# Four-layer graph network: layer 1 prepared in three blocks beside layer 0's output projection, and row norms applied without their scale

## The chip, the core and the metric

The program runs on one core of one Trainium2 chip. A core has five engines that each work through their own instructions in order: PE (TensorE, matrix products and transposes; its weight loads are shown as PEld), DVE (VectorE), ACT (ScalarE), POOL (GpSimd) and SP (SyncE, which here issues DMAs). They wait for each other through semaphores. PE writes to eight PSUM banks; everything else is in SBUF or in the chip's main memory. The metric is the device time of one execution in microseconds (us); lower is better.

## The reference

The input is `x`, 3327 nodes of 128 features, and `adj`, a sparse weighted 3327 x 3327 matrix. Four layers follow each other, each of them as `x = x + layer(relu(layernorm(x)), adj)`; the norm has no weights: `(x - mean) / sqrt(var + 1e-5)`.

- Layer 0: attention with 128 heads of 8 features, with 2 x `adj` added to the scores before the softmax, and an output projection with `Wo`.
- Layer 1 (hyperbolic): `h = exp0(log0(x) @ embed)`, a hyperbolic addition of a bias, `neigh = exp0(adj @ log0(h))`, then the same kind of product with `layer` on `[x, neigh]`. `exp0` and `log0` scale each row by a function of its length (`tanh(n)/n`, `artanh(n)/n`), so every row needs the sums of squares of several vectors.
- Layer 2 (hyperbolic): `adj @ logmap0(...)` on rows made in the same manner from `x @ weight.T` and a bias, with clips to the ball.
- Layer 3: `A_norm @ X @ W_in + A.T_norm @ X @ W_out`, each with the inverse degrees of its direction.

So layers 1 to 3 need four products of `adj` (or its transpose) with a 3327 x 128 matrix.

## The kernel before

**Attention (to about 10281 us).** Scores, exponentials and products for 128 heads; the result goes to main memory as `oT_d`, 9 values per head and node: 8 sums and the softmax's denominator. The change does not touch this part.

**The last part** works on 26 tiles of 128 nodes (`NT = 26`), kept in SBUF as `xs`. Two blocks, `BLOCKS = (range(0, 16), range(16, 26))`, are prepared one after the other.

*Output projection* (lines 1095 to 1115). For each tile, `f_load` brings 9 x 128 x 128 values from `oT_d` (odd tiles on POOL's queue, even ones on SP's) to one of four buffers `f_ot`, which borrow space in `uT` and `w1`. `f_norm` divides by the denominators on DVE (a reciprocal and a product, L1101 and L1102), `f_turn` makes eight transposes on PE (L1108) that ACT copies back (L1109), and `f_mul` makes eight products with `woT` (L1114), whose sum DVE adds to `xs` (L1115). The loop at line 1317 issues the norm two tiles ahead and the turn one tile ahead of the product. `load_nodes` (line 830) loads all of `x` on SP between the first tile loads.

*Chains.* Work beside the main loops is written as generators. `start` puts one in a list, `tick(us)` lets the first of the list issue its next pieces until their stated costs (the numbers that they yield) have used up `us`, and `drain` issues the rest at once. This decides at build time where an instruction stands on each engine; at run time every engine takes its own in that order.

*Preparing a block* (`pre1` for layer 1, `pre2` for layer 2): statistics of each tile on DVE (`layer_norm`, L926 and L927), the inverse deviation `r`, `relu(r x - r mean)` per tile on ACT (L933), squares on ACT and their sums on DVE (`row_squares`, L917 and L919), a chain of some 25 small DVE operations on `[128, tiles]` with a square root and a logarithm on ACT, transposes of the tiles by PE (L941) and copies to `hT` by DVE (L942), products with the layer's weight (`project`, L961), whose result `take_a` copies and squares on ACT, a second chain of some 45 small operations with four functions on ACT, and `spread` (L974 and L912), which makes the tiles `y`. ACT loads a table before a function of another set (L185).

*Aggregation* (`aggregate`, line 1021). For each of 26 strips of 128 rows of `adj` or its transpose, PE multiplies tile `y[t]` with the strip's chunks of 512 columns (L1035), and `tick` follows every chunk. In some aggregations DVE also sums the strip for the degrees (L1039). `feed` loads strips into a pool of six buffers, on SP and POOL in turns. A strip's buffer is free once PE and the degree sum are through with it.

The order is: projection with `pre1` of block 0 beside it and drained after it; aggregation of layer 1 over block 0's columns, with `pre1` of block 1 beside it, drained before strip 16; its second half, with `post1` and `pre2` of block 0 beside it, drained after it; layer 2's first half with `post1` and `pre2` of block 1 beside it, drained before strip 16; and so on to layer 3. The lines that set the start of layer 1 are these:

```python
        if t == first[-1]:
            drain()
            start(pre1(0))
        tick(1.1)
        if t >= NT - 4:
            feed(t - NT + 5)
```

## Time and profile before

| | us |
|---|---|
| median of 3 runs (11112.82 to 11114.44) | 11113.94 |
| the profiled execution | 11115.08 |
| its span | 11113.3 |
| output projection's first transposes of a tile | 10297.90 |
| first aggregation's first product | 10429.53 |
| PE waits before layer 2's first product | 15.30, until 10621.68 |
| PE waits before strip 16 of that aggregation | 14.22, until 10701.16 |

The page gives busy times over the whole span: ACT 10187.7 us (92%), PE 10706.3 (96%), DVE 8565.0 (77%). These are mostly the attention's. For the part that the change touches, stretches of the last 832 us have to be asked for. In a timeline a line has the start, the time that a run of equal instructions took, the engine, the line of the kernel, the operation, what it writes and reads, their number, and in brackets how long the engine was idle before it and who ended that. `SPq` is SP's queue of DMA issues. An `issue` in brackets means that the profile shows no wait that ended there. Starts of following lines tell the cadence, which is shorter than the durations where instructions overlap. A transpose or a product may be recorded in one or two pieces, so counts are twice the number of products for L1114, L961 and L1035.

### The profile page before, as it was taken

The page shows a single profiled execution, that of the slowest core. Times are in us where ns is not written, and L with a number is a line of the kernel's source. Part 1 is how long each engine was busy: PE and PEld are TensorE (multiplying, and loading weights), DVE is VectorE, ACT ScalarE, POOL GpSimd, SP SyncE. Part 2 cuts the span into 40 slices and gives each one's busy share as a digit, 9 for nine tenths or more (in the row PEclk, how much of TensorE's full clock was granted, in tenths as well). Part 3 has the DMA queues.
Part 4 walks back from the last instruction along what each step waited for, and adds up shares of the span by engine and source line. Part 5 has one row for each costly group of instructions (what it writes and reads, how often), then busy time and mean ns, then how long its engine had stood idle before and what let it go on. Part 6 is the DMA issues. An engine that isn't in the chain of part 4 may idle for free. (4 is left out here: it accounts for less than half of the span.)

```text
span 11113.3 us, 205604 instructions
## 1 busy us (share of the span) xinstructions
PE 10706.3 (96%) x72876; PEld 3602.0 (32%) x72876; DVE 8565.0 (77%) x13863; ACT 10187.7 (92%) x13845; POOL 2014.2 (18%) x3149
## 2 busy tenths in 40 slices
PE   4599999999999999999999999999999999999889
PEld 2233333333333333333333333333333333333544
DVE  5588887888878887788887888878887777777655
ACT  3599999999999999999999999999999999999330
POOL 5111111111111111111111111111111111111101
PEclk7799999999999999999999999999999999999899
DMA  8855555555555554555555555565555554443668
GB/s 248 253 95 90 96 96 103 97 96 88 96 110 90 95 96 78 110 96 88 96 88 112 96 96 86 90 119 89 94 88 88 104 85 80 84 84 65 195 234 281
DMA packets 683025, 1243.40 MB, mean 112 GB/s; under 512 B 188050, under 2 KB 543401, under 8 KB 668943
## 3 DMA queue, kind: packets, MB, share of 16 engines
q1 hardware_dynamic: 631724, 1100.76, 51.5%
q0 software_dynamic: 50272, 129.37, 4.1%
q8 instruction: 590, 9.67, 0.4%
q14 instruction: 439, 3.60, 0.2%
HBM read 1082.90 MB, written 146.60 MB: 111 GB/s over the span
## 5 line engine op out<-in xcount | busy, mean ns | idle before, releaser
L659 ACT ACTIVATE e<-S 128x952 f32<-128x952 f32 (+1 forms) x9408 | 8702.4, 1150 | 13.0 <-PE S L647 10.4
L700 PE MATMUL po<-e,VA 128*9 128x476 f32 (+1 forms) x46592 | 5738.4, 564 | 19.8 <-DVE OS L708 2.9
L640 DVE TENSOR_TENSOR S<-a,shb 128x476 f32<-128x476 f32 (+1 forms) x5824 | 4026.9, 691 | 1769.4 <-ACT e L659 1307.6
L647 PE MATMUL S<-QS,KT 64*128 64x476 f32 (+1 forms) x23296 | 4841.3, 447 | 50.5 <-DVE S L640 24.3
L647 PEld LDWEIGHTS S<-QS,KT 64*128 64x128 f32 x23296 | 2410.1, 183 | 5143.4 <-ACT e L659 1473.3
L662 ACT ACTIVATE e<-S 128x476 f32<-128x476 f32 (+1 forms) x3808 | 2363.0, 760 | 3.8 <-PE S L647 3.5
L682 DVE SCALAR_TENSOR_TENSOR e<-e,h 128x476 f32<-128x476 f32 (+1 forms) x2016 | 1388.3, 689 | 46.2
L712 POOL DMA_DIRECT2D oT_d<-OS x896 | 470.8, 531 | 4788.5 <-DVE OS L708 4742.9
L566 POOL TENSOR_SCALAR QS<-QS 32x476 fp32r<-32x476 f32 (+1 forms) x1344 | 986.6, 734 | 1470.0 <-DMA QS<-qS_d 798.3
L700 PEld LDWEIGHTS po<-e,VA 128*9 128x9 f32 x46592 | 690.8, 88 | 1607.3 <-issue 1514.0
L1035 PE MATMUL pu<-strip,y 128*128 128x512 f32 (+2 forms) x1456 | 600.6, 567 | 44.8 <-issue 29.2
L673 DVE TENSOR_SCALAR h<-S 128x476 f32<-128x476 f32 (+1 forms) x672 | 439.1, 653 | 78.7 <-PE S L647 5.6
L684 DVE SCALAR_TENSOR_TENSOR e<-e,h 128x476 f32<-128x476 f32 (+1 forms) x672 | 442.7, 659 | 0.0
L677 DVE TENSOR_TENSOR h<-h,h 128x476 f32<-128x476 f32 (+1 forms) x672 | 442.5, 658 | 0.0
L682 DVE SCALAR_TENSOR_TENSOR e<-h 128x476 f32<-128x476 f32 (+1 forms) x672 | 438.9, 653 | 0.0
L576 POOL COPY VA<-VR 128x832 f32<-128x832 f32 x224 | 223.6, 998 | 958.2 <-DMA VR<-v_d 644.9
L1035 PEld LDWEIGHTS pu<-strip,y 128*128 128x128 f32 (+1 forms) x1456 | 272.9, 192 | 322.4 <-issue 288.5
L675 DVE TENSOR_SCALAR h<-h 128x476 f32<-128x476 f32 (+1 forms) x672 | 318.7, 474 | 23.2
L679 DVE TENSOR_SCALAR h<-h 128x476 int32<-128x476 f32 (+1 forms) x672 | 279.2, 415 | 23.0
L1039 DVE TENSOR_REDUCE deg<-strip 128x1 f32<-128x1536 f32 (+3 forms) x104 | 192.8, 1881 | 77.7 <-DMA strip<-in_adj_dram 41.0
L987 ACT COPY uT<-pu 128x512 f32<-128x512 f32 (+1 forms) x21 | 11.2, 553 | 244.3 <-PE pu L1035 244.3
L291 DVE STREAM_TRANSPOSE cols<-rows 128x416 f32<-128x416 f32 x208 | 204.3, 987 | 21.2 <-DMA rows<-in_adj_dram 13.6
(240 smaller groups left out, 2050.6 us busy)
## 6 DMA issues: line engine op xcount, KB each, us to landing
KT<-kS_d SPq DMA_DIRECT2D x1792, 208.0 KB
KT<-kS_d SPq DMA_DIRECT2D x1792, 104.0 KB
VR<-v_d SPq DMA_DIRECT2D x224, 416.0 KB
QS<-qS_d SPq DMA_DIRECT2D x3072, 14.9 KB
QS<-qS_d SPq DMA_DIRECT2D x1536, 29.8 KB
adjT<-cols SPq DMA_DIRECT2D x26, 1664.0 KB
a<-adjT SPq DMA_DIRECT2D x156, 238.0 KB
rows<-in_adj_dram SPq DMA_DIRECT2D x309, 104.0 KB
```

The source lines that it names most:

```text
L566: nc.gpsimd.tensor_scalar(QS[b][r0:r0 + 32, j + 1, :w], QS[b][r0:r0 + 32, j, :w].bitcast(F32), -1.0, 0.0, op0=ALU.mult, op1=ALU.add)
L640: touch(u, [r], nc.vector.tensor_tensor(bank(u, r), adj_of[c][2 * q + r][:, :w], shift_of[c][:, :w], op=ALU.subtract))
L647: x = nc.tensor.matmul(bank(u, r), KT[b][64 * r:64 * r + 64, max(0, j - 1), q * P:(q + 1) * P], QS[b][64 * r:64 * r + 64, j, :w], start=Fa ...
L659: touch(u, (0, 1), nc.scalar.activation(e[:, :, :w], S[:, odd:even + 1, :w], AF.Exp, scale=2.0))
L662: touch(u, [r], nc.scalar.activation(e[:, 1 - r, :w], bank(u, r), AF.Exp, scale=2.0))
L673: touch(u, [1], nc.vector.tensor_scalar(f, bank(u, 1), LOG2_E2, EXP_LEAST, op0=ALU.mult, op1=ALU.max))
L677: nc.vector.tensor_tensor(f, f, whole, op=ALU.subtract)
L682: nc.vector.scalar_tensor_tensor(e, f if k == 4 else e, EXP_C[k], f, op0=ALU.add, op1=ALU.mult)
L684: nc.vector.scalar_tensor_tensor(e, e, EXP_C[0], power.bitcast(F32), op0=ALU.add, op1=ALU.mult)
L700: nc.tensor.matmul(po[32 * j:32 * j + H + 1, :w], VA[k % 2][:, 2 * pairs[v][2] + of, j, :], e_of[v, j][:, 1 - of, :w], start=(q == 0 and r ...
L712: nc.gpsimd.dma_start(oT_d[:, d * N + c * CW:d * N + c * CW + w], o[32 * j:32 * j + H + 1, :w])
L1035: nc.tensor.matmul(got[c][:, :k], y[:m, t, :], s[:m, c * 4 * P - c0:c * 4 * P - c0 + k], start=(t == 0), stop=(t == NT - 1))
```

## The change

- The norm of layers 1 and 2 is made by a new function `centred` in place of `layer_norm`, `squared` and `turned`. DVE only subtracts the mean and clips at zero; the scale `r` is left out, and put in later, on small values: sums of squares are multiplied by `r * r`, the projection's dot product and the coefficient of `a` by `r`, and the copies of the other projection (`keep1`) by `r` of their row. Every four tiles it transposes, copies to `hT` on ACT and squares. In `pre2` the additions of `post1` are made inside the same loop, tile by tile.
- `pre1` is run for tiles 0 to 7, 8 to 15 and 16 to 25. The first two are started at the projection's tiles 7 and 15, and the loop's `tick` is 3.5 in place of 1.1.
- The projection has eight tile buffers; four are strips' buffers, borrowed from the pool of six. Tile loads and node loads are issued in another order, and strips are fed from three tiles before the end of the loop instead of four.
- `row_squares` becomes `square_of`: the sum over a group's squares is issued after the next group's square. Its tile has six buffers.

`layer_norm` stays in use for layer 3.

```diff
-    def load_nodes():
-        nc.gpsimd.memset(xs[96:P, NT - 1, :], 0.0)
-        nc.sync.dma_start(xs[:, 0:13, :], node_rows(x, 0, 13))
-        nc.sync.dma_start(xs[:, 13:NT - 1, :], node_rows(x, 13, NT - 1))
-        for p0, p1 in pieces(P - 1):
-            nc.sync.dma_start(xs[p0:p1, NT - 1, :], x[(NT - 1) * P + p0:(NT - 1) * P + p1])
+    def load_nodes(t0, t1):
+        m = min(t1, NT - 1)
+        nc.sync.dma_start(xs[:, t0:m, :], node_rows(x, t0, m))
+        if t1 == NT:
+            nc.gpsimd.memset(xs[96:P, NT - 1, :], 0.0)
+            for p0, p1 in pieces(P - 1):
+                nc.sync.dma_start(xs[p0:p1, NT - 1, :], x[(NT - 1) * P + p0:(NT - 1) * P + p1])
...
-    def row_squares(sm, dst, ts, rows):
-        sq = part.tile([P, 4, P], F32, name="sq")
+    late = deque()
+    def reduce_late(k=0):
+        while len(late) > k:
+            late.popleft()()
+    def square_of(ts, rows, sm, dst):
+        sq = part.tile([P, 4, P], F32, name="sq", bufs=6)
         nc.scalar.activation(sq[:, :len(ts), :], rows, AF.Square)
         t0 = sm.own[0]
-        nc.vector.tensor_reduce(dst[:, ts[0] - t0:ts[-1] + 1 - t0], sq[:, :len(ts), :], axis=AX.X, op=ALU.add)
+        late.append(lambda: nc.vector.tensor_reduce(dst[:, ts[0] - t0:ts[-1] + 1 - t0], sq[:, :len(ts), :],
+                                                    axis=AX.X, op=ALU.add))
+        reduce_late(1)
...
-    def turned(h):
-        def go(ts):
+    def centred(sm, h, add=None):
+        ts = sm.own
+        mv = wts.tile([P, len(ts), 2], F32, name=f"{sm.pre}_mv")
+        sm.hh = sm.new()
+        for four in fours(ts):
+            for t in four:
+                if add:
+                    add(t)
+                st = part.tile([P, 6], F32, name="st", bufs=8)
+                nc.vector.bn_stats(st, xs[:, t, :])
+                nc.vector.bn_aggr(mv[:, t - ts[0], :], st)
+                nc.vector.tensor_scalar(h[:, t, :], xs[:, t, :], mv[:, t - ts[0], 0:1], 0.0, op0=ALU.subtract, op1=ALU.max)
+                yield 1.4 if add else 0.7
             ps = next_bank()
-            for t in ts:
-                nc.tensor.transpose(ps[:, (t - ts[0]) * P:(t - ts[0] + 1) * P], h[:, t, :], ident)
-            nc.vector.tensor_copy(hT[:, columns(ts)], flat(ps, ts))
-        return go
-    def squared(sm, h):
-        o = sm.new()
-        for ts in fours(sm.own):
-            row_squares(sm, o, ts, nodes(h, ts))
-            yield 0.8
-        sm.last = o
+            for t in four:
+                nc.tensor.transpose(ps[:, (t - four[0]) * P:(t - four[0] + 1) * P], h[:, t, :], ident)
+            nc.scalar.copy(hT[:, columns(four)], flat(ps, four))
+            square_of(four, nodes(h, four), sm, sm.hh)
+        reduce_late()
+        sm.r = sm.recip(sm.sqrt(sm.ts(mv[:, :, 1], LN_EPS, ALU.add)))
+        sm.r2 = sm.mul(sm.r, sm.r)
+        sm.hh = sm.mul(sm.hh, sm.r2)
...
             yield 1.0
+        reduce_late()
     def take_a(sm, aa):
         def take(ts, ps):
             nc.scalar.copy(nodes(a, ts), ps)
-            row_squares(sm, aa, ts, ps[:, :, 0:D])
+            square_of(ts, ps[:, :, 0:D], sm, aa)
         return take
...
         "p (e i) -> p e i", e=H + 1) for i in range(2)]
+    f_ot += [strips.tile([P, 16 * P], F32, name="strip")[:, 0:9 * P].rearrange("p (e i) -> p e i", e=H + 1)
+             for i in range(4)]
     woT = uT[:, 18 * P:26 * P].rearrange("p (e o) -> p e o", e=H)
...
+    f_load(0)
+    f_load(1)
     nc.sync.dma_start(wo, Wo)
-    for t in range(2):
+    f_load(2)
+    load_nodes(0, 4)
+    for t in range(3, 7):
         f_load(t)
-    load_nodes()
-    for t in range(2, 4):
-        f_load(t)
+    load_nodes(4, NT)
     eb, lb, hb = on_all(embed_bias, "eb"), on_all(layer_bias, "lb"), on_all(bias, "hb")
...
         nc.scalar.copy(woT[:, k0:k0 + 4, :].rearrange("p e o -> p (e o)"), ps)
-    state = {}
-    def pre1(b):
-        sm = state["p", b] = Part(f"p{b}", BLOCKS[b])
+    hh_all, r_all = (wts.tile([P, NT], F32, name=n) for n in ("hh_all", "r_all"))
+    def pre1(ts):
+        sm = Part(f"p{ts[0]}", ts)
         h = ys[0]
-        yield from layer_norm(sm, h)
-        yield from squared(sm, h)
-        sm.hh = sm.last
+        yield from centred(sm, h)
         nx = sm.ts(sm.sqrt(sm.hh), L1_EPS, ALU.max)
         s1 = sm.div(sm.artanh(nx, L1_MAX_TANH), nx)
-        for ts in fours(sm.own):
-            turned(h)(ts)
-            yield 1.0
+        nc.vector.tensor_copy(hh_all[:, ts[0]:ts[-1] + 1], sm.hh)
+        nc.vector.tensor_copy(r_all[:, ts[0]:ts[-1] + 1], sm.r)
         yield cost() * 0.3
         aa = sm.new()
         yield from project(sm, hT, emb_w, take_a(sm, aa))
+        aa, ab = sm.mul(aa, sm.r2), sm.mul(nodes(a, ts)[:, :, D], sm.r)
         an = sm.sqrt(aa)
         nv = sm.ts(sm.mul(s1, an), L1_EPS, ALU.max)
         c1 = sm.div(sm.mul(sm.act(nv, AF.Tanh), s1), nv)
-        ab = nodes(a, sm.own)[:, :, D]
         eb2 = sums[0]
         al, be = ball_sum(sm, c1, aa, ab, eb2, L1_EPS)
         yn = sm.ts(sum_norm(sm, al, be, aa, ab, eb2), L1_EPS, ALU.max)
         f = sm.div(sm.artanh(yn, L1_MAX_TANH), yn)
-        al, be = sm.mul(al, f), sm.mul(be, f)
+        al, be = sm.mul(sm.mul(al, sm.r), f), sm.mul(be, f)
         yield cost() * 0.5
         yield from spread(sm, ys[0], al, be, eb)
-    def keep1(b):
-        def take(ts, ps):
-            nc.scalar.copy(nodes(w1, ts), ps)
-        yield from project(state["p", b], hT, lay_w[0], take)
+    def keep1(ts):
+        def take(own, ps):
+            for t in own:
+                nc.scalar.activation(w1[:, t, :], ps[:, t - own[0], :], AF.Copy, scale=r_all[:, t:t + 1])
+        yield from project(Part("k", ts), hT, lay_w[0], take)
     def post1(b, got):
-        sm, was = Part(f"q{b}", BLOCKS[b]), state["p", b]
+        sm = Part(f"q{b}", BLOCKS[b])
         yield from received(sm, got)
...
                 add_scaled(w1[:, t, :], ps[:, t - ts[0], :], sm.at(cu, t), w1[:, t, :])
-            row_squares(sm, ww, ts, nodes(w1, ts)[:, :, 0:D])
+            square_of(ts, nodes(w1, ts)[:, :, 0:D], sm, ww)
         yield cost() * 0.6
         yield from project(sm, uT, lay_w[1], take)
         gn = sm.mul(cu, uu)
-        nz = sm.ts(sm.sqrt(sm.add(was.hh, sm.mul(gn, gn))), L1_EPS, ALU.max)
+        nz = sm.ts(sm.sqrt(sm.add(nodes2(hh_all, sm.own), sm.mul(gn, gn))), L1_EPS, ALU.max)
         sz = sm.div(sm.artanh(nz, L1_MAX_TANH), nz)
         wn = sm.sqrt(ww)
         nv2 = sm.ts(sm.mul(sz, wn), L1_EPS, ALU.max)
         c2 = sm.div(sm.mul(sm.act(nv2, AF.Tanh), sz), nv2)
         al, be = ball_sum(sm, c2, ww, nodes(w1, sm.own)[:, :, D], sums[1], L1_EPS)
         yield cost()
-        for t in sm.own:
+        def add(t):
             add_scaled(xs[:, t, :], w1[:, t, 0:D], sm.at(al, t), xs[:, t, :])
             add_scaled(xs[:, t, :], lb, sm.at(be, t), xs[:, t, :])
-            yield 0.4
+        added[b] = add
+    added = {}
     def pre2(b):
         sm = Part(f"r{b}", BLOCKS[b])
         h = ys[1]
-        yield from layer_norm(sm, h)
-        yield from squared(sm, h)
-        xn = sm.ts(sm.sqrt(sm.last), L2_MIN_NORM, ALU.max)
+        yield from centred(sm, h, added[b])
+        xn = sm.ts(sm.sqrt(sm.hh), L2_MIN_NORM, ALU.max)
         ax = sm.div(sm.artanh(xn, L2_MAX_TANH), xn)
-        for ts in fours(sm.own):
-            turned(h)(ts)
-            yield 1.0
         yield cost() * 0.3
         aa = sm.new()
         yield from project(sm, hT, w2T, take_a(sm, aa))
+        aa, ab = sm.mul(aa, sm.r2), sm.mul(nodes(a, sm.own)[:, :, D], sm.r)
         an = sm.ts(sm.sqrt(aa), L2_MIN_NORM, ALU.max)
         th = sm.act(sm.mul(an, ax), AF.Tanh)
         c1 = sm.mul(sm.div(th, an), clip_of(sm, sm.ts(th, L2_MIN_NORM, ALU.max)))
-        ab = nodes(a, sm.own)[:, :, D]
         hb2 = sums[2]
         al, be = ball_sum(sm, c1, aa, ab, hb2, L2_MIN_NORM)
         yn = sm.ts(sum_norm(sm, al, be, aa, ab, hb2), L2_MIN_NORM, ALU.max)
         pf = clip_of(sm, yn)
         pn = sm.ts(sm.mul(yn, pf), L2_MIN_NORM, ALU.max)
         f = sm.mul(sm.div(sm.artanh(pn, L2_MAX_TANH), pn), pf)
-        al, be = sm.mul(al, f), sm.mul(be, f)
+        al, be = sm.mul(sm.mul(al, sm.r), f), sm.mul(be, f)
         yield cost() * 0.5
...
             nc.scalar.activation(u, flat(ps, ts).rearrange("p (t o) -> p t o", o=D), AF.Relu)
-            row_squares(sm, rr, ts, u)
+            square_of(ts, u, sm, rr)
             yield 1.0
+        reduce_late()
         t1 = sm.ts(sm.act(un, AF.Tanh), L2_MIN_NORM, ALU.max)
...
     f_turn(0)
+    f_load(7)
     for t in range(NT):
         if t + 2 < NT:
             f_norm(t + 2)
         if t + 1 < NT:
             f_turn(t + 1)
-        if t + 4 < NT:
-            f_load(t + 4)
+        if t + 8 < NT:
+            f_load(t + 8)
         f_mul(t)
-        if t == 5:
+        if t == 4:
             start(prepare())
-        if t == first[-1]:
-            drain()
-            start(pre1(0))
-        tick(1.1)
-        if t >= NT - 4:
-            feed(t - NT + 5)
+        if t == 7:
+            start(pre1(range(0, 8)))
+        if t == 15:
+            start(pre1(range(8, 16)))
+        tick(3.5)
+        if t >= NT - 3:
+            feed(t - NT + 4)
     nc.gpsimd.memset(uT[:, N:NP], 0.0)
...
     use(7, 4, 5, 6)
-    ready = start(pre1(1))
-    start(keep1(0))
-    start(keep1(1))
+    ready = start(pre1(second))
+    start(keep1(first))
+    start(keep1(second))
     got = aggregate(ys[0], first, 0, ready=ready, deg=deg[0], deg_w=final[0][0] * P)
```

## The prediction

> **What bounds the kernel.** I read the page's slices first: up to about 10281 us ScalarE's exponentials fill the span, and the change touches nothing there. All that it edits runs in the last 832 us. For these I read the windows, then PE's timeline for its idle time, then DVE's for the work behind each gap.
>
> Windows of the last stages; the columns are the stretch, its length, then busy us (instructions) of PE, PEld, DVE, ACT and POOL, PE's clock, DMA share, GB/s:
>
> ```profile
> 10302.00:10398.00 96.00, 79.13 (x617) 76.94 (x618) 70.11 (x143) 34.35 (x64) 13.08 (x15) 0.90 0.69 209
> 10398.00:10430.00 32.00, 9.69 (x51) 7.97 (x50) 21.43 (x94) 19.14 (x42) 0.63 (x2) 0.70 0.09 34
> 10430.00:10531.00 101.00, 100.52 (x290) 48.98 (x290) 71.83 (x163) 29.94 (x69) 6.87 (x13) 0.98 0.67 238
> ...
> 10594.00:10622.00 28.00, 8.50 (x51) 8.03 (x50) 20.80 (x98) 13.53 (x28) 0.00 (x0) 0.64 0.29 123
> ...
> 10737.00:11113.00 376.00, 368.49 (x1067) 187.09 (x1065) 203.66 (x335) 47.98 (x88) 40.87 (x77) 1.00 0.81 278
> ```
>
> From 10737 on PE is full, so a shift before it is carried to the end. What can be won lies in three places: the output projection with layer 1's first preparation (10302 to 10430), the gap at 10594, and one at 10687. PE's timeline shows what ended the gaps:
>
> ```profile
> 10332.47 1.94 PE L1108 MATMUL pu<-ident,uT 128*128 128x128 f32 x8 [2.99 <-issue]
> ...
> 10343.54 1.94 PE L1108 MATMUL pu<-ident,w 128*128 128x128 f32 x8 [4.16 <-issue]
> ...
> 10393.55 1.06 PE L1108 MATMUL pu<-ident,uT 128*128 128x128 f32 x8 [1.90 <-issue]
> ...
> 10429.53 16.38 PE L1035 MATMUL pu<-strip,y 128*128 128x512 f32 x32 [13.86 <-issue]
> ...
> 10621.68 5.58 PE L1035 MATMUL pu<-strip,y 128*128 128x512 f32 x8 [15.30 <-issue]
> ...
> 10701.16 4.25 PE L1035 MATMUL pu<-strip,y 128*128 128x512 f32 x6 [14.22 <-DVE y L912]
> ```
>
> DVE's timeline names the work: one projection tile, and the late loads and lumps that interrupt it:
>
> ```profile
> 10309.23 0.95 DVE L1101 RECIPROCAL y<-w 128x128 f32<-128x128 f32 x1 [7.20 <-DMA w<-oT_d]
> ...
> 10336.76 0.29 DVE L1115 TENSOR_TENSOR xs<-xs,pu 128x128 f32<-128x128 f32 x1 [2.07 <-PE pu L1114]
> ...
> 10348.93 0.29 DVE L1115 TENSOR_TENSOR xs<-xs,pu 128x128 f32<-128x128 f32 x1 [3.17 <-PE pu L1114]
> ...
> 10380.30 0.92 DVE L1101 RECIPROCAL y<-w 128x128 f32<-128x128 f32 x1
> 10381.25 1.23 DVE L1102 TENSOR_TENSOR w<-w,y 128x1024 f32<-128x1024 f32 x1
> 10382.39 0.28 DVE L1115 TENSOR_TENSOR xs<-xs,pu 128x128 f32<-128x128 f32 x1
> ...
> 10404.54 0.17 DVE L170 TENSOR_SCALAR p<-p 128x16 f32<-128x16 f32 x1
> ...
> 10409.21 2.48 DVE L942 COPY hT<-pu 128x512 f32<-128x512 f32 x4
> ...
> 10460.10 0.17 DVE L170 TENSOR_SCALAR p<-p 128x10 f32<-128x10 f32 x1
> ...
> 10470.43 5.06 DVE L1039 TENSOR_REDUCE deg<-strip 128x1 f32<-128x1536 f32 x3
> ```
>
> The reader is to see that a projection tile costs DVE 0.97 + 1.14 + 0.20 = 2.3 us from start to start, against about 2.7 on PE (eight transposes 0.95, eight products 1.79). DVE has some room, but not for everything that the change puts there. The last four lines bound a first chain (from 10404.54 to the copies) and a second one (from 10460.10 to the degree sum).
>
> **Step 1, eight tile buffers.** Tile 2's load left SP only at 10302.48, behind the loads of the node rows, and DVE waited 7.20 us for it. Issued ahead of most of those rows, it lands with tile 1 (about 10300). PE loses a gap of 4.08 us and part of a slow restart; tile 2's add would end at 10314.4 in place of 10318.9, so -4.5 (0 if the load is no earlier, -7.2 if all of the wait counts). Node rows 4 to 25 now go behind tiles 4 and 6 on SP; the fifth tile's add needs them near 10320, and SP was through with all its node rows at 10302 in this trace, so I give that nothing. On POOL the weights' loads now stand behind three tile loads of 1.0 us, one more than before; their first reader starts past 10320, so that costs nothing either (about 1 if DVE came there at once).
>
> **Step 2, layer 1 in blocks beside the projection.** Before, DVE needed one chain for 16 tiles, mostly behind the projection. Now two blocks of 8 each carry the whole chain, and a small operation on 10 columns (0.17) costs what one on 16 does. DVE per block:
> - eight tiles of statistics (0.40 from start to start) and the new subtract-and-clip, 128x128, each after the statistics that it reads: 0.35, by the scaling of hb, 0.29 long and 0.33 to the next start (0.2 if it overlaps as the adds do): 6.0;
> - two reductions of squares, 1.2;
> - first chain: 1.6 (10388.81 to 10390.42), 4.7 (10404.54 to 10409.21), four new small operations 0.8: 7.1;
> - three reductions of `aa`, 1.3;
> - second chain, from the ten-column row 10460.10 to 10470.43: 10.3, and three new multiplies 0.6: 10.9;
> - eight y tiles at 0.296: 2.4.
>
> That is 28.9 per block, 57.8 for two. From tile 2's add on DVE also does 21 norms x 2.11 and 23 adds x 0.20, 48.9, and the weights' preparation 3.1 + 4.3 + 0.85 = 8.2. After the last norm PE still has one turn and two products, 4.4. Without any wait: 119.3.
>
> Waits come on top. DVE issues a chain as one lump of 7 to 11 us, and each following norm is queued behind it. PE gets one tile ahead, then idles until norms return, and restarts slowly: after the 2.99 and 4.16 gaps eight transposes took 1.94, after 1.90 only 1.06. The lumps of 3.1 and 4.3 us cost 2.07 and 3.17 at the add. Two longer lumps per block, at 2.0 on average because reductions and y tiles fill part of it, give 8; the last square of each group has to go PE, ACT, ACT, DVE (rows 0.6, 0.55, 0.6, less the reduction that covers some), 1.2 twice per block, 4.8; the weights' lump, now one, 2.6; PE-paced tiles 0.6. Together 16 (5 if PE's restarts cost nothing; 26 with the longest gap, 4.16, for each lump).
>
> The first aggregation then starts at 10314.4 + 119.3 + 16 = 10449.7, against 10429.5: **+20.2** (+4 with waits of 5, the cheap clip and all of the 7.20; +35 with waits of 26 and no gain from the loads). Projection and preparation no longer stand one after the other, yet DVE, busy 91.5 of these 128 us and idle the rest, gets a second chain (about 18), the clips (16 x 0.35) and loses only the hT copies (2.5).
>
> The Trainium skill (TensorE: Matmul & The Clock Gate, Part 1) puts the fall to half clock after an idle window of about 3.4 us. By it the 2.99 gap might have been harmless; here it was not. All four lumps leave PE idle for longer than that, so the sum is the same by the page and by the rows.
> The Trainium skill (ScalarE: Activation LUTs, What ACT_TABLE_LOAD costs) counts a drain of 1.38 us behind each 1.28 us load; six loads per block would make that, as an estimate from the page, 16.6 us more, and the result 11148. In this trace a load takes 1.28, and DVE waits 0.28 behind most of them, so the sum goes without.
>
> **Step 3, first aggregation.** PE stays busy over the last projection tiles, so the slow first strip (5.9 us instead of 3.4) is saved: -2.5. Against it, the third block's last transposes now stand 7 us into the aggregation, and ten tiles of clip, a degree sum (1.7) and a reduction need DVE 10 us: PE waits about 2.5. Sum 0 (-3 if PE never waits, +4 if the clips take longer). Strips: two fit beside the four borrowed buffers, and the others follow as tiles 20 to 23 are turned, over 8 us ahead.
>
> **Step 4, gap at 10594.** Relu on ACT (6.3) and the copies on DVE go from this path, and the products now follow the transposes at once. But the last transposes still stand at the end of the aggregation, now ahead of ACT's copy 0.55, square 0.55, reduction 0.62, and of both square roots: 5.2 until the logarithm, behind which ACT's `a` copies queue. They would begin near 10602.5, against 10601.94 before, and run faster (4.4 for 5.6); three multiplies give 0.6 back. Taken as 0 (-4 if the roots overlap the copies, +4 if the last transposes wait for DVE).
>
> **Step 5, gap at 10687.** Same parts on ten tiles. Additions and clips end near 10667.2 (10653.2 + 10 x 1.4), the logarithm near 10678.7, last `aa` near 10683.8 against 10687.7; with 0.6 of multiplies -3.3 (-6 to 0, as the clip is cheap or PE holds the transposes back). Later reductions, scaled copies of w1 (26 x 0.3 on ACT) and post2 lie under full PE: nothing; if that cover went, ACT's copies would cost some 4.
>
> **Sum.** -4.5 is inside the 20.2; 20.2 + 0 + 0 - 3.3 = +16.9. The profiled execution took 11115.1 (span 11113.3, 1.8 around it), 1.1 over the median of the runs. 11113.9 + 16.9 gives 11131 us.
>
> **Rivals.** (a) Waits mostly vanish, PE restarts warm (waits 5, clip hidden in 0.2): the start moves +7, the rest -5: about 11116, no change. DVE's busy 73% in the projection speaks for room, the 2.07 and 3.17 against. (b) Faster by over 22 us, below 11092: the start would have to come before 10422 and both gaps lose 15 together. DVE alone, without any wait, ends at 10434; so it needs small operations half as dear on 8 columns as on 10 (18 us). 16 columns and 10 show 0.17 both. (c) Slower than 11136: each lump costs 4 or more, or the deeper lumps hold back degree sums, so strips come late in the first aggregation; it decides once waits pass 21 us. 11142. (d) The tiles' loads were the pace, at 0.69 DMA share, and the change only smooths them: the -4.5 and -3.3 alone, 11106, if DVE's second chain hid fully; the DVE count excludes most of it.
>
> **Numbers.** Forecast (waits 8 to 21) 0.47, (a) 0.19, (c) 0.27, (d) 0.03, (b) 0.04. The bound of 0.2%, about what can be told here, is 22 us: below 11092 or above 11136. Of the forecast 0.03 lies beyond that (its other terms at their upper ends), so slower 0.30; faster 0.04; same 0.66. All lower bounds together give 11105, all upper ones 11157; the range goes from 11104, just under (d), to 11146, above (c), and leaves out (b) and the worst of (c).
>
> **What would show it.** Right: first L1035 strip at 10445 to 10455 of after; DVE over 80% busy from 10302 to there; adds that wait 2 us for PE after each chain; no wait over 1 us for tile 2; gap at the next block unchanged within 4 us; the one at strip 16 near 11. Wrong: a first strip before 10435, a clip under 0.2 us, or strips waiting for DMA or degree sums in the first aggregation.

## The result, and the profile after

| | before | after |
|---|---|---|
| median of 16 runs, us | 11115.72 (11112.76 to 11120.43) | 11138.08 (11133.93 to 11144.62) |
| the profiled execution, us | 11115.08 | 11135.88 |
| its span, us | 11113.3 | 11134.1 |

The ratio is 1.0020, with a 95% interval of 1.0012 to 1.0028: the change makes the kernel 22.4 us slower. The forecast was +16.9 us, 11131.

In the profiled executions the last part begins at different times, so all stages below are counted from the attention's last DVE copy (10284.83 us before, 10282.81 after).

| stage, us | before | after | difference | forecast |
|---|---|---|---|---|
| last attention copy to tile 2's add | 33.88 | 30.60 | -3.3 | -4.5 |
| tile 2's add to the first aggregation's first product | 110.82 | 144.11 | +33.3 | +24.7 |
| first aggregation, first half | 101.65 | 100.90 | -0.7 | 0 |
| its second half and the gap behind it | 90.51 | 89.79 | -0.7 | 0 |
| layer 2, first half, with the wait at strip 16 | 115.33 | 110.99 | -4.3 | -3.3 |
| the rest | 376.30 | 374.91 | -1.4 | 0 |
| sum | 828.49 | 851.30 | +22.8 | +16.9 |

One term carries the error: the second line came out 8.6 us too long. The rest is within 1.4 us each.

Windows of the kernel after; the columns are the stretch, its length, then busy us (instructions) of PE, PEld, DVE, ACT and POOL, PE's clock, DMA share, GB/s:

```profile
10302.00:10400.00 98.00, 57.57 (x396) 54.58 (x397) 71.53 (x218) 35.77 (x67) 9.22 (x10) 0.80 0.52 146
10400.00:10457.50 57.50, 37.11 (x247) 35.98 (x246) 38.47 (x135) 24.47 (x48) 2.13 (x3) 0.77 0.26 89
10457.50:10558.40 100.90, 99.29 (x292) 48.49 (x291) 70.61 (x162) 26.88 (x66) 7.54 (x15) 1.00 0.68 249
10620.00:10648.20 28.20, 7.14 (x45) 5.55 (x44) 19.35 (x103) 15.38 (x30) 0.53 (x1) 0.70 0.38 161
10759.20:11134.00 374.80, 368.07 (x1067) 187.18 (x1065) 203.46 (x335) 47.89 (x88) 41.05 (x77) 1.00 0.81 278
```

The first two lines are the projection with both blocks of layer 1. DVE is the busiest engine there, but it is busy only 110.0 of 155.5 us, 71%, where the forecast wanted over 80%. PE's granted clock is 0.80 and 0.77. So neither engine is full: they wait for each other. PE's timeline of the kernel after shows where the idle time lies, and the two later gaps, now 17.31 and 9.20 us; its first two lines follow the first block's clips:

```profile
10342.14 1.91 PE L1131 MATMUL pu<-ident,uT 128*128 128x128 f32 x8
10343.84 2.33 PE L1137 MATMUL pu<-uT,y 128*128 128x128 f32 x16
...
10379.95 1.94 PE L1131 MATMUL pu<-ident,strip 128*128 128x128 f32 x8 [11.60 <-issue]
10381.68 3.62 PE L1137 MATMUL pu<-uT,y 128*128 128x128 f32 x16
10385.10 1.28 PE L1131 MATMUL pu<-ident,strip 128*128 128x128 f32 x8
10386.22 1.95 PE L1137 MATMUL pu<-uT,y 128*128 128x128 f32 x16
...
10457.52 3.60 PE L1056 MATMUL pu<-strip,y 128*128 128x512 f32 x8
...
10648.20 5.47 PE L1056 MATMUL pu<-strip,y 128*128 128x512 f32 x8 [17.31 <-issue]
...
10722.66 2.93 PE L1056 MATMUL pu<-strip,y 128*128 128x512 f32 x3 [9.20 <-DVE y L916]
```

DVE's timeline of the kernel after, at the start of the projection, behind the first block's clips, around the end of a second chain, and at the third block's statistics and clips:

```profile
10303.92 0.95 DVE L1124 RECIPROCAL y<-w 128x128 f32<-128x128 f32 x1 [5.05 <-DMA w<-oT_d]
...
10320.75 0.29 DVE L1138 TENSOR_TENSOR xs<-xs,pu 128x128 f32<-128x128 f32 x1 [2.19 <-DMA xs<-in_x_dram]
...
10335.39 0.29 DVE L1138 TENSOR_TENSOR xs<-xs,pu 128x128 f32<-128x128 f32 x1 [2.40 <-PE pu L1137]
...
10346.20 0.29 DVE L1138 TENSOR_TENSOR xs<-xs,pu 128x128 f32<-128x128 f32 x1 [1.53 <-PE pu L1137]
...
10377.20 0.52 DVE L158 TENSOR_TENSOR p<-p,p 128x8 f32<-128x8 f32 x4
10377.64 0.95 DVE L1124 RECIPROCAL y<-strip 128x128 f32<-128x128 f32 x1
10378.62 1.23 DVE L1125 TENSOR_TENSOR strip<-strip,y 128x1024 f32<-128x1024 f32 x1
10379.77 0.28 DVE L1138 TENSOR_TENSOR xs<-xs,pu 128x128 f32<-128x128 f32 x1
10379.97 0.94 DVE L1124 RECIPROCAL y<-strip 128x128 f32<-128x128 f32 x1
10380.94 1.23 DVE L1125 TENSOR_TENSOR strip<-strip,y 128x1024 f32<-128x1024 f32 x1
10385.34 0.29 DVE L1138 TENSOR_TENSOR xs<-xs,pu 128x128 f32<-128x128 f32 x1 [3.17 <-PE pu L1137]
...
10395.65 0.29 DVE L959 BATCH_NORM_STATS2 st<-xs 128x6 f32<-128x128 f32 x1
10395.97 0.18 DVE L960 BATCH_NORM_AGGREGATE p_mv<-st 128x2 f32<-128x6 f32 x1
10396.18 0.29 DVE L961 TENSOR_SCALAR y<-xs,p_mv 128x128 f32<-128x128 f32 x1
10396.39 0.28 DVE L959 BATCH_NORM_STATS2 st<-xs 128x6 f32<-128x128 f32 x1
```

The first of these waits is for tile 2, the second for the node rows of the fifth tile, the third stands behind the weights' lump. SP's queue in the kernel after shows why the rows came late: tiles 4 and 6 held the queue for 10.36 us ahead of them:

```profile
10290.58 10.36 SPq L1119 DMA_DIRECT2D strip<-oT_d  x2
10301.15 5.47 SPq L832 DMA_DIRECT2D xs<-in_x_dram  x1
```

The lines from 10377.20 to 10385.34 of DVE's timeline show the pattern of the stage. While the chain runs on DVE, PE finishes the tile that it has and idles 11.60 us. When the chain ends (10377.6), DVE normalises a tile, adds the one that PE had finished, normalises the next tile, and then wants the sum of a tile that PE could begin only at 10379.95, after the first of these norms. PE needs the turn, ACT's copy and the products for it, and runs them at about half speed after its idle time: 1.94 and 3.62 us, against 1.04 and 1.95 later. So DVE waits 3.17 us at the second add behind each second chain, and 2.7 us behind each first one. Behind the five clips of a block that one tick issues it is the first add that waits (1.53 and 1.86 us), for another reason: PE takes its work in order, and ahead of this add's products stand the transposes of the clipped tiles, which wait for DVE, and the next tile's turn. This turn and the products then take 1.91 and 2.33 us, the first two lines of PE's timeline. All waits of DVE from tile 2's add to the first aggregation, apart from those inside the chains and at the last two adds, which the forecast had counted with the work:

| wait of DVE, us | forecast | measured |
|---|---|---|
| adds behind the blocks' lumps | 8 (two per block at 2.0) | 15.1 (three per block: 1.53, 2.69, 3.17; 1.86, 2.70, 3.17) |
| add behind the weights' lump | 2.6 | 2.4 |
| last squares of a group | 4.8 | 3.2 |
| other adds paced by PE | 0.6 | 2.2 |
| fifth tile's add, for its node rows | 0 | 2.2 |
| sum | 16 | 25.1 |

144.1 - 25.1 = 119.0 us is left for the work, against 119.3 in the forecast.

### The profile page after: what moved, and what is told of

Read it like the earlier page. It is cut to its first block, busy times and chain, and to the rows that moved or that the text cites. A ratio compares the mean times of both kernels' runs of the same rounds, so it can differ in the third digit from the quotient of the medians.

```text
span 11134.1 us, 205731 instructions
## 1 busy us (share of the span) xinstructions
PE 10704.3 (96%) x72876; PEld 3601.1 (32%) x72876; DVE 8599.6 (77%) x14005; ACT 10186.3 (91%) x13836; POOL 2008.9 (18%) x3149
## 5 line engine op out<-in xcount | busy, mean ns | idle before, releaser
L1056 PE MATMUL pu<-strip,y 128*128 128x512 f32 (+2 forms) x1456 | 599.1, 566 | 27.5 <-issue 17.3
L291 DVE STREAM_TRANSPOSE cols<-rows 128x416 f32<-128x416 f32 x208 | 204.5, 988 | 21.1 <-DMA rows<-in_adj_dram 13.2
```

What stands on the lines that cost most here:

```text
L1056: nc.tensor.matmul(got[c][:, :k], y[:m, t, :], s[:m, c * 4 * P - c0:c * 4 * P - c0 + k], start=(t == 0), stop=(t == NT - 1))
```

## The experiments

Theory A: DVE's work, with the waits that the written order puts behind its lumps, sets the start of the first aggregation; the forecast's error is the size of these waits. Its rivals were that the waits are PE's own pace and only move, and that loads, clips or the transposes in single file are the cause. The stages of all runs, cut as above, in us:

| run | to tile 2's add | from there to the first aggregation | first half | second half, gap | layer 2, first half | rest | sum |
|---|---|---|---|---|---|---|---|
| before | 33.88 | 110.82 | 101.65 | 90.51 | 115.33 | 376.30 | 828.5 |
| after | 30.60 | 144.11 | 100.90 | 89.79 | 110.99 | 374.91 | 851.3 |
| one block | 28.66 | 115.76 | 104.33 | 89.63 | 112.44 | 375.85 | 826.7 |
| three blocks | 27.51 | 154.55 | 100.89 | 89.62 | 110.82 | 374.99 | 858.4 |
| three tiles ahead | 30.17 | 125.44 | 100.89 | 89.62 | 111.90 | 375.31 | 833.3 |
| node rows 0 to 7 early | 31.36 | 142.37 | 100.89 | 89.77 | 111.01 | 375.03 | 850.4 |
| before + buffers | 27.72 | 112.62 | 101.64 | 90.68 | 115.43 | 376.02 | 824.1 |
| before + layer 2's norm | 37.42 | 111.04 | 101.64 | 89.63 | 111.97 | 375.67 | 827.4 |
| chains in pieces | 30.96 | 122.54 | 105.22 | 89.81 | 110.85 | 375.60 | 835.0 |
| pieces, three ahead | 31.07 | 112.18 | 105.23 | 89.79 | 110.90 | 375.64 | 824.8 |
| combined | 30.76 | 102.16 | 103.43 | 89.64 | 111.31 | 375.83 | 813.1 |
| combined, weights early | 35.84 | 90.55 | 103.43 | 89.64 | 111.47 | 375.64 | 806.6 |
| the same, rows on POOL | 35.87 | 90.62 | 103.43 | 89.65 | 111.41 | 375.48 | 806.5 |
| squares at once | 27.88 | 146.47 | 107.84 | 96.22 | 117.06 | 376.13 | 871.6 |

The first column is partly chance: the nine runs with the changed kernel's loads and the weights behind tile 4 or 5 have 27.5 to 31.1, and the two with the loads of before, which are the same there, 33.9 and 37.4. Where a run leaves that part alone, the second column is the better one to compare.

**One block for tiles 0 to 15.**

```diff
-        if t == 7:
-            start(pre1(range(0, 8)))
-        if t == 15:
-            start(pre1(range(8, 16)))
+        if t == 15:
+            start(pre1(first))
```

> The changed kernel, with tiles 0 to 15 of layer 1 prepared as one block (from tile 15 on) in place of two blocks of 8; all else as changed. Counted from the attention's last DVE copy, the first aggregation started after 174.7 us in the changed kernel and after 144.7 in the kernel before. Theory A (the mis-sized term is the waits: each block costs its two chains on DVE, measured 6.7 + 10.8 = 17.5, and the waits behind its lumps, measured 1.5 + 1.0 + 2.7 + 0.4 + 3.2 + 0.5 = 9.2): one block less brings the start to 174.7 - 26.7 = 148.0, up to 5 later if the only second chain ends after the last tile, uncovered; total near 11111 to 11116. Rival B (only DVE's work counts, the waits are PE's pace and come back elsewhere): 174.7 - 17.5 = 157.2, total near 11121. Rival C (the blocks are not the cause; loads, clip and transposes in single file are): 170 to 175, total near 11137.

Measured: the start at 144.4, against 148.0 by theory A and 157.2 by work alone. The median is 11114.35, a ratio of 0.9997 (0.9988 to 1.0007) to the kernel before. From tile 2's add 28.4 us go: DVE's busy time in that stretch falls by 14.2 (103.2 to 89.0) and its waits of 0.15 us or more by 10.9; the other 3.3 lie in shorter gaps and behind the last add. The second block is what made the change slower. From tile 2's add the stretch is still 4.9 us longer than before; the start is as early because tile 2 comes earlier. The larger `tick` and the later `feed` were not tested alone; this run keeps both. Of its 28.4 us, 3.4 come back in the first aggregation, where the last y tiles are still being made.

**Three blocks.**

```diff
-        if t == 7:
-            start(pre1(range(0, 8)))
-        if t == 15:
-            start(pre1(range(8, 16)))
+        if t == 5:
+            start(pre1(range(0, 6)))
+        if t == 10:
+            start(pre1(range(6, 11)))
+        if t == 15:
+            start(pre1(range(11, 16)))
```

> The changed kernel, with tiles 0 to 15 prepared in three blocks (6, 5 and 5 tiles) in place of two of 8: one pair of chains and one more set of lumps. Theory A: the first aggregation starts at 174.7 + 17.5 + 9.2 = 201 us after the attention's last DVE copy, total near 11164. Rival B (work alone): 192, total near 11155. Rival C (the number of blocks does not matter): 175 to 178, total near 11139.

Measured: 182.1, ratio 1.0028 (1.0018 to 1.0038). Theory A missed by 19 us and the rival by 10. From tile 2's add it is +10.4. The work did come: DVE's busy time rises by 13.2, from 103.2 to 116.4 (a small operation takes 0.17 on 6 columns as on 8 or 16). But the idle time falls by 3.6: the adds' waits for PE are 13.6 in place of 17.5, and DVE waited 0.3 for the squares in place of 3.2. DVE's timeline of this run, behind a first chain:

```profile
10355.32 0.16 DVE L1203 COPY r_all<-p 128x6 f32<-128x6 f32 x1
10355.39 0.95 DVE L1124 RECIPROCAL y<-w 128x128 f32<-128x128 f32 x1
10356.37 1.22 DVE L1125 TENSOR_TENSOR w<-w,y 128x1024 f32<-128x1024 f32 x1
10357.51 0.28 DVE L1138 TENSOR_TENSOR xs<-xs,pu 128x128 f32<-128x128 f32 x1
10357.71 0.54 DVE L929 TENSOR_REDUCE p<-sq 128x3 f32<-128x384 f32 x1
```

Here one norm and one add follow the chain, the add finds its sum ready, and the second chain comes at once behind it. The exposed second add comes once for both chains. So a wait is not a price per block: it depends on what follows a lump in the order.

**Tiles normalised three ahead.**

```diff
     f_norm(1)
+    f_norm(2)
     f_turn(0)
...
-        if t + 2 < NT:
-            f_norm(t + 2)
+        if t + 3 < NT:
+            f_norm(t + 3)
```

> The changed kernel, with tiles normalised three ahead of their product in place of two; the same work in the same blocks. In the changed kernel the adds waited 17.5 us in all for PE in the second place behind each lump: 2.40, 1.53, 2.69, 3.17, 1.86, 2.70, 3.17. Theory A (the wait is PE's latency from a norm through turn, copy and product, on a PE that has gone slow, and only the order of norm and add exposes it): with one more tile normalised before each lump, two adds behind it find their product done and the third waits 0.9 at most; waits fall from 17.5 to about 5, the first aggregation starts at 174.7 - 12 = 163, total near 11126. Rival B (the waits are the pace of PE and ACT and only move): 172 to 176, total near 11138.

Measured: 155.6, 19.1 earlier than in the changed kernel; median 11119.80, ratio 1.0001 (0.9991 to 1.0011). The work is the same. PE's and then DVE's timeline of this run, around the end of a second chain:

```profile
10420.27 3.78 PE L1137 MATMUL pu<-uT,y 128*128 128x128 f32 x16 [8.42 <-ACT y L1132]
10424.35 1.42 PE L1131 MATMUL pu<-ident,strip 128*128 128x128 f32 x8 [0.30 <-PE pu L1137]
10425.61 1.95 PE L1137 MATMUL pu<-uT,y 128*128 128x128 f32 x16
```

```profile
10421.61 0.52 DVE L158 TENSOR_TENSOR p<-p,p 128x8 f32<-128x8 f32 x4
10422.05 0.95 DVE L1124 RECIPROCAL y<-strip 128x128 f32<-128x128 f32 x1
10423.03 1.23 DVE L1125 TENSOR_TENSOR strip<-strip,y 128x1024 f32<-128x1024 f32 x1
10424.17 0.28 DVE L1138 TENSOR_TENSOR xs<-xs,pu 128x128 f32<-128x128 f32 x1
10424.37 0.95 DVE L1124 RECIPROCAL y<-strip 128x128 f32<-128x128 f32 x1
10425.35 1.23 DVE L1125 TENSOR_TENSOR strip<-strip,y 128x1024 f32<-128x1024 f32 x1
10426.49 0.28 DVE L1138 TENSOR_TENSOR xs<-xs,pu 128x128 f32<-128x128 f32 x1
```

PE still idles 8.42 us and still restarts slowly (3.78 for the products), but no add waits behind the chain: DVE has two adds whose products PE can make without a norm from behind the lump. The idle and slow PE cost nothing here by themselves; they cost where the order makes DVE ask for their result at once. Waits at the adds fell by more than the 12 expected, and those for squares also fell, from 3.2 to 1.9. What is left before the last adds, 1.86 and 2.83, stands behind the clips, where PE's own order holds the products back and one more norm ahead does not help.

**Node rows 0 to 7 early.**

```diff
-    load_nodes(0, 4)
+    load_nodes(0, 8)
...
-    load_nodes(4, NT)
+    load_nodes(8, NT)
```

> The changed kernel, with node rows 0 to 7 loaded where rows 0 to 3 were (behind tile 2), and rows 8 to 25 behind tiles 4 and 6. In the changed kernel the fifth tile's add waited 2.19 us for its node rows, which left the queue only at 10301. Theory A (that wait is a term of its own, which the forecast put at nothing): it goes, and the first aggregation starts 2.2 earlier, near 172.5, total near 11136. Rival B (loads only change places: tiles 4 and 6 arrive later and their norms wait instead): 174 to 177, total 11138 to 11140.

Measured: 173.7, 1.0 earlier in the profile; ratio 1.0020 (1.0010 to 1.0029), not to be told from the changed kernel. The fifth tile's wait went, but now the first tile's add waits (DVE's timeline of this run):

```profile
10312.03 0.29 DVE L1138 TENSOR_TENSOR xs<-xs,pu 128x128 f32<-128x128 f32 x1 [4.61 <-DMA xs<-in_x_dram]
```

The rival is right for the most part: the first tiles' data come as fast as the transfers bring them, and another order moves the wait.

**The buffers alone.** The kernel before with eight tile buffers and the changed order of loads:

```diff
+    f_ot += [strips.tile([P, 16 * P], F32, name="strip")[:, 0:9 * P].rearrange("p (e i) -> p e i", e=H + 1)
+             for i in range(4)]
...
+    f_load(0)
+    f_load(1)
     nc.sync.dma_start(wo, Wo)
-    for t in range(2):
-        f_load(t)
-    load_nodes()
-    for t in range(2, 4):
+    f_load(2)
+    load_nodes(0, 4)
+    for t in range(3, 7):
         f_load(t)
+    load_nodes(4, NT)
```

> The kernel before with the eight tile buffers and the new order of the loads alone. Theory A (as the changed kernel's trace has it): tile 2's add comes 3.3 us earlier, the fifth tile's add then waits about 2.2 us for its node rows, so the first aggregation starts 1 to 3 us earlier than before (144.7 after the attention's last DVE copy): 142 to 144, total near 11114. Rival B (tile loads were the pace of the projection, rival (d) of the forecast): 135 to 139, total near 11108. Rival C (the later node rows cost more than the earlier tile brings): 146 to 149, total near 11118.

Measured: the start at 140.4, 4.3 earlier, of which tile 2's add gives 6.2 and the wait for node rows takes part back; the sum of stages is 4.4 lower. The ratio, 0.9997 (0.9988 to 1.0006), cannot show that, and the first column varies by some 3.5 us between runs with the same loads. The same wait stands here as in the changed kernel (DVE's timeline of this run):

```profile
10326.46 0.29 DVE L1118 TENSOR_TENSOR xs<-xs,pu 128x128 f32<-128x128 f32 x1 [3.92 <-DMA xs<-in_x_dram]
```

**Layer 2's norm alone.** The kernel before, with `centred` and late sums in `pre2` only:

```diff
-        yield from layer_norm(sm, h)
-        yield from squared(sm, h)
-        xn = sm.ts(sm.sqrt(sm.last), L2_MIN_NORM, ALU.max)
+        yield from centred(sm, h, added[b])
+        xn = sm.ts(sm.sqrt(sm.hh), L2_MIN_NORM, ALU.max)
...
-        for ts in fours(sm.own):
-            turned(h)(ts)
-            yield 1.0
...
+        aa, ab = sm.mul(aa, sm.r2), sm.mul(nodes(a, sm.own)[:, :, D], sm.r)
```

> The kernel before with the norm applied without its scale, and squares summed late, in layer 2's preparation alone. In the changed kernel the stretch from layer 2's first aggregation to its second half was 111.0 us against 115.3, the gap ahead of it 0.7 shorter, the last stretch 374.9 against 376.3. Theory A (these gains belong to this part): 5 to 6 us less in all, total near 11109, first aggregation's start unchanged at 144.7. Rival B (they came from layer 1's side: scaled w1, earlier squares, other bank order): 0 to -2, total near 11113.

Measured, by stages: -0.9, -3.4 and -0.6 in the last three, 4.9 in all, so about three quarters of the changed kernel's gain in these stretches (6.5) is this part's. The wait at strip 16 is as short as there (PE's timeline of this run):

```profile
10702.54 18.05 PE L1079 MATMUL pu<-strip,y 128*128 128x512 f32 x35 [9.18 <-DVE y L912]
```

The ratio, 0.9998 (0.9989 to 1.0007), leaves it open: the interval reaches 10 us to either side. The start at 148.5, where 144.7 was expected, comes from tile 2's load, which this run does not change; from tile 2's add on it takes 111.0, as before.

**Chains in pieces.** Yields inside the chains of `centred` (layer 1) and `pre1`, so that norms and adds come between:

```diff
         sm.hh = sm.mul(sm.hh, sm.r2)
+        if not add:
+            yield 2.0
...
         nx = sm.ts(sm.sqrt(sm.hh), L1_EPS, ALU.max)
+        yield 1.5
...
         an = sm.sqrt(aa)
+        yield 2.0
...
         eb2 = sums[0]
+        yield 2.0
         al, be = ball_sum(sm, c1, aa, ab, eb2, L1_EPS)
+        yield 2.0
         yn = sm.ts(sum_norm(sm, al, be, aa, ab, eb2), L1_EPS, ALU.max)
+        yield 2.0
```

> The changed kernel with yields inside the two chains, so that norms and adds come between pieces of 2 to 3 us; the same work. Theory A (length of the lump sets the wait at the adds): the waits behind the chains, 2.69 and 3.17 in each block, fall to under 1 each, and part of the waits for ACT is covered; first aggregation at 164 to 168 after the attention's last DVE copy against 174.7, total near 11129. Rival B (every lump costs its wait, whatever its length; three blocks showed that the wait hangs on the place in the order): 172 to 180, total near 11140.

Measured: the start at 153.5, 21.2 earlier; median 11125.27, ratio 1.0008 (0.9999 to 1.0017). Most waits behind the chains are gone; DVE's timeline of this run, between the two chains of the first block:

```profile
10364.33 0.94 DVE L1126 RECIPROCAL y<-strip 128x128 f32<-128x128 f32 x1
10365.31 1.22 DVE L1127 TENSOR_TENSOR strip<-strip,y 128x1024 f32<-128x1024 f32 x1
10366.46 0.28 DVE L1140 TENSOR_TENSOR xs<-xs,pu 128x128 f32<-128x128 f32 x1
10366.65 0.55 DVE L929 TENSOR_REDUCE p<-sq 128x3 f32<-128x384 f32 x1
10367.12 0.94 DVE L1126 RECIPROCAL y<-strip 128x128 f32<-128x128 f32 x1
10368.09 1.22 DVE L1127 TENSOR_TENSOR strip<-strip,y 128x1024 f32<-128x1024 f32 x1
10369.53 0.29 DVE L1140 TENSOR_TENSOR xs<-xs,pu 128x128 f32<-128x128 f32 x1 [0.22 <-PE pu L1139]
```

Where the changed kernel's add waited 2.69, it now waits 0.22. One wait of 3.09 is left, behind the first block's second chain, whose last pieces still run for 5.7 us without a norm between them. The gain was larger than expected. But 4.3 us come back in the first aggregation: the stretched chain leaves the second block's y tiles behind the last add, the third block's clips come later on DVE, and PE, whose transposes of them stand in front of the strips, takes 8.2 us for the first strip in place of 3.9.

**Both remedies in the changed kernel.** The edits of the last run and of the third tile together:

> The changed kernel (two blocks of 8) with both remedies: chains in pieces, and tiles normalised three ahead. From tile 2's add to the first aggregation the changed kernel took 144.1 us, the pieces alone 122.6, the third tile alone 125.4; the forecast's count of DVE's work without any wait was 119.3. Theory A (what is left is DVE's work, so the count is a floor that both remedies approach and do not pass): 117 to 121; with 105 for the aggregation, as with the pieces alone, a total near 11122. Rival B (each remedy removes its own waits, and the count was too high): 105 to 112, total near 11112. Rival C (another engine or the loads hold it): 122 or more.

Measured: 112.2 from tile 2's add, ratio 0.9994 (0.9985 to 1.0004). DVE's idle time there is 10.3 us in place of 32.9. It lies between the two theories, 5 below A's lower end and at B's upper one: 4.3 of the work went into the first aggregation, one norm (2.2 us) now stands ahead of tile 2's add, and the forecast's count held the waits for ACT inside the chains (about 5 us), which the pieces now cover in part. The count was thus no floor. The changed kernel, with all its blocks, is then level with the kernel before, so what made it slower can be taken away without taking work away.

**Combined.** One block of 16 whose clips follow the projection's tiles, with both remedies:

```diff
+        if t == 8:
+            start(pre1(first))
-        if t == 7:
-            start(pre1(range(0, 8)))
-        if t == 15:
-            start(pre1(range(8, 16)))
-        tick(3.5)
+        tick(1.4 if 7 < t < 15 else 3.5)
```

> The changed kernel with one block of 16 tiles whose statistics and clips follow the tiles two at a time from tile 8 on, the chains in pieces, and tiles normalised three ahead. Theory A (DVE's work, and waits that the order makes, set the start): one block alone measured 144.4 after the attention's last DVE copy; its waits for PE behind lumps were 2.1 + 1.8 + 1.6 + 2.1 = 7.6, of which about 6 go, and 2 for ACT: 136, with 101 for the aggregation in place of 104; total near 11104. Rival B (with the chains paid once, PE, ACT or the tiles' loads set the pace): 142 to 145, total near 11112.

Measured: 132.9, median 11100.79, ratio 0.9986 (0.9977 to 0.9995). It beats both kernels.

**Weights prepared right behind tile 0's add.**

```diff
-        if t == 4:
+        if t == 0:
             start(prepare())
```

> One block, statistics following the tiles, chains in pieces, three tiles ahead, and the weights prepared right behind tile 0's add instead of tile 4's. In the run without that last step DVE was idle 4.2 + 1.4 + 1.1 + 1.5 us for loads of the first tiles, and the weights' preparation (8.2 on DVE) stood behind them. Theory A (the idle time of the loads takes up about half of it): first aggregation at 127 to 130 after the attention's last DVE copy against 132.9, total near 11096. Rival B (the weights land too late, or the loads, not DVE, set the first tiles): 132 to 136, total near 11101.

Measured: the start at 126.4, ratio 0.9980 (0.9971 to 0.9989): about 22 us faster than the kernel before. The kernel before ran at 11128.33 in this comparison, against 11114.79 in the one before it, so the ratio is the number to keep. The weights' lump now fills time in which DVE waited for loads: the first column grows by 5.1, the second falls by 11.6. Windows of this run, from tile 2's add to the first aggregation:

```profile
10322.00:10412.50 90.50, 72.83 (x576) 70.01 (x575) 78.81 (x219) 42.10 (x85) 8.16 (x9) 0.92 0.55 164
```

DVE is busy 87% and PE's clock is 0.92, against 0.77 to 0.80 in the changed kernel.

**Node rows 4 to 12 on POOL's queue,** ahead of the weights:

```diff
     for t in range(3, 7):
         f_load(t)
-    load_nodes(4, NT)
+        if t == 5:
+            load_nodes(4, 13, nc.gpsimd)
+    load_nodes(13, NT)
```

> As the run with the weights prepared behind tile 0's add, and node rows 4 to 12 loaded on the queue of the odd tiles (ahead of the weights) instead of behind tiles 4 and 6. Theory A (a wait of an add for its node rows, 1.5 us, goes): first aggregation 1 to 2 earlier than in that run, total near 11095. Rival B (the weights, now behind the node rows, come later, and DVE waits for them in the first tiles): 1 to 4 later, total near 11098.

Measured: 126.5 and a sum of 806.5 against 806.6, ratio 0.9977 (0.9968 to 0.9986). Neither gain nor loss: once the weights' lump stands in front of the fifth tile's add, the rows have come.

**Squares summed at once.** The changed kernel with one edit:

```diff
-        reduce_late(1)
+        reduce_late(0)
```

> The changed kernel with every reduction of squares issued right behind its square, in place of a group later. In the changed kernel DVE waited 1.0 + 0.4 us per block for the last squares (the forecast had put 2.4 on them). Theory A (the late sum saves a wait of about 1.0 at each of the three other groups of a block): from tile 2's add to the first aggregation 144.1 + 6 = 150, layer 2 another 2 to 3 longer, total near 11146. Rival B (the time that DVE waits there is time that it would wait for PE at the next add anyway): 144 to 146, layer 2 unchanged within 1, total near 11138.

Measured: median 11160.21, ratio 1.0038 (1.0024 to 1.0053): 20.3 us more in the stages. From tile 2's add to the first aggregation it is only 2.4, as rival B had it. The rest was expected in that size by neither: +6.9, +6.4 and +6.1 in the three stretches behind it. DVE's and then PE's timeline of this run, in layer 2's preparation and in the first aggregation:

```profile
10619.93 0.69 DVE L929 TENSOR_REDUCE r<-sq 128x4 f32<-128x512 f32 x1 [5.49 <-ACT sq L927]
...
10628.25 0.69 DVE L929 TENSOR_REDUCE r<-sq 128x4 f32<-128x512 f32 x1 [1.57 <-ACT sq L927]
```

```profile
10474.80 0.48 PE L965 MATMUL pu<-ident,y 128*128 128x128 f32 x1 [2.07 <-DVE y L961]
```

A reduction at once makes DVE wait until PE has come to the group's transposes in its own order, and ACT to the copy and the square: 5.49 us and then 1.57 for each group. All clips behind it come that much later, and PE, which takes its transposes in order, holds up strips for them. Full PE is then no cover: it is PE that waits.

## Why the prediction was right, and where it was not

- **What bounds it, and the sign.** Right. The second block's chains on DVE in the projection decide the result; one block brings the start back to that of the kernel before, with tile 2's earlier load.
- **DVE's work (119.3 without waits).** Right as a sum, 119.0 by difference: 109.9 us of work, and 9.1 of waits for ACT in the chains and the weights' preparation and for PE at the last adds, which the forecast had counted with it. First chain 6.7 us (forecast 7.1), second 10.8 (10.9). The clip was put at 0.35 and takes 0.20 from start to start, but the statistics ahead of it, put at 0.40, take 0.54. Two errors cancel: a tile's statistics and clip repeat every 0.74 us, against 0.75. "Wrong: [...] a clip under 0.2 us" stood on the edge and moved nothing.
- **The total.** 11131 against 11138, in the range, which ended at 11146; 1.8 of these 7 us lie in the kernel before, whose median is 11115.72 in 16 runs and was 11113.94 in three; the interval of the ratio lies on both sides of the 0.2% that the chances were given for. The first strip came at 10457.5, behind the 10445 to 10455 that was to show the forecast right, though the last part had begun 2.0 us earlier. DVE was busy 71% up to there, not over 80%.
- **Waits (16).** This is the step that failed in size: 25.1. It counted two lumps per block at 2.0; there were three, because the five clips issued in one tick are a lump too (1.5 and 1.9), and the two chains cost 2.7 and 3.2. The forecast took 2.0 on average "because reductions and y tiles fill part of it"; the runs showed that at the second add behind a chain they fill little of it: this add carries what the one norm ahead of it leaves of the latency of turn, copy and products on a slow PE. The node rows' 2.2, put at nothing, and 1.6 more at other adds came on top, and the squares took 1.6 less. By the forecast's own bound ("it decides once waits pass 21 us") rival (c) is what came, and its 11142 missed by 4 us where the forecast missed by 7. But no single lump cost the 4 that (c) named; three per block made 7.4 and 7.7. Its other mechanism did not come: PE is busy 99.3 of the first aggregation's 100.9 us, so no strip was late.
- **Clock.** Confirmed in the new gaps: after 11.60 us without work eight transposes took 1.94 and products 3.62. The gaps behind the four chains, 5.23 to 11.60 us, all lie beyond the 3.4 us that the Trainium skill (TensorE: Matmul & The Clock Gate, Part 1) gives for the fall. Shorter gaps in the runs do not sort by their length: with the chains in pieces, eight transposes took 1.06 us behind a gap of 3.00 (at 10309.40) and 1.94 behind one of 2.37 (at 10318.44), each from full speed, so the length of one gap does not decide by itself. That the slow restart costs only where an add stands behind it was not in the forecast. The drain behind each table load (the Trainium skill, ScalarE: Activation LUTs, What ACT_TABLE_LOAD costs), which by the forecast's estimate would have added 16.6 us, is not in the runs: in the changed kernel a load that starts at 10367.92 takes 1.28 us, and the activation behind it starts at 10369.22.
- **Loads (-4.5; "no wait over 1 us for tile 2").** The direction held, -3.3 here and -6.2 with the buffers alone, in single profiles, but DVE still waited 5.05 us for tile 2. "Node rows 4 to 25 [...] I give that nothing" was wrong: 2.19 us here, 3.92 with the buffers alone. The trace of before had all node rows issued by 10302; moved behind tiles 4 and 6 they were not issued before 10301.
- **Steps 3 and 4 (0 each).** -0.7 each. They are near nothing only because the sums of squares are late: at once, they are +6.2 and +5.7 against the kernel before. The forecast gave late sums no such worth.
- **Step 5 (-3.3).** -4.3, and the wait at strip 16 9.20 where 11 was forecast. The rest, put at nothing, gave -1.4.
- **The sum.** 8.6 too little in one term, 0.7 + 0.7 + 1.0 + 1.4 too much in the others, 1.2 on the loads: +22.8 in the stages in place of +16.9. The parts of the change that gain are the buffers (4 us) and layer 2's norm with late sums (5 us), by the stages of one profile each, which the ratios are too wide to confirm; with these, one block and another order, the last part is 22 us shorter than before instead of 23 longer.

## What to carry to other kernels

Count a lump of instructions twice: once for its own time, and once for the first later instruction on its engine that needs a result which another engine could only start after the lump; one more stage of lead, or cutting the lump where neighbours can pass, takes most of that second price away without less work. Behind the clips, where PE's transposes stand in the way, one more stage did not. When work is spread beside another loop, splitting it into blocks multiplies everything whose cost does not depend on the block's size, here 17.5 us per pair of chains, their waits for ACT included. And an instruction that waits for a result of two other engines belongs one group later, above all where the engines behind it work strictly in order.

## What the runs showed of the hardware

A dependent small DVE operation on 5, 6, 8, 10 or 16 columns takes 0.17 us and starts 0.20 after the one before it (a reciprocal 0.19 to 0.25 long). One DMA issue can hold its queue long: on SP the issues of tiles 4 and 6 together took 10.4 us in the changed kernel, and those of node rows 4 to 24 and of the last tile's rows 5.5 and 9.8 more, where the first tiles' issues took 0.4. The time to the first tiles varies by several us between runs with the same loads (27.5 to 31.1), so a gain of 5 us is only seen when counted from behind them.
